# GpSimd multiplies the fourth corner by its weight in every second tap of a deformable convolution's sampling

## The chip, the cores and the metric

The kernel runs on one core of one Trainium2 chip. The metric is the time of one execution on the device, in microseconds (us). Three executions of the kernel before took 7953.55, 7961.13 and 7967.98 us; their median is 7961.13 us. A further one was recorded by the hardware profiler, and all views of the profile come from it.

## The reference

The program is two layers of a vision model on an input of 2 x 128 x 64 x 64 numbers, all float32: a deformable convolution with four branches, a mixture of experts, a state-space mixer and a second mixture of experts, each with a residual. The change lies in the sampling of the deformable convolution. For each branch (kernel sizes 1, 1, 3 and 7) and each of its taps, every output position reads the normalized image at a position that is not whole, as a weighted sum of four neighbours, and the result goes into a product with the tap's weights:

```python
v00 = gather(y0, x0)
v01 = gather(y0, x0 + 1)
v10 = gather(y0 + 1, x0)
v11 = gather(y0 + 1, x0 + 1)
return v00 * (1 - wy) * (1 - wx) + v01 * (1 - wy) * wx + v10 * wy * (1 - wx) + v11 * wy * wx
...
sampled = bilinear_sample(x, py, px) * mask[:, None]
return jnp.einsum('bckhw,ock->bohw', sampled, reg_w.reshape(O, C, k * k))
```

1 + 1 + 9 + 49 = 60 taps are sampled at 4096 positions of each of the two images. The offsets and masks that fix positions and weights come from convolutions of the same image.

## The kernel before

The image lies in device memory as a table (`self.table`) of 67 x 67 rows; a row holds the 4 x 128 channels of the four neighbours of one position, so one gathered row of 2 KB is all that a position needs of a tap. Positions go in groups of 512 (`NG` = 8 groups for an image), a group in `GT` = 4 tiles of 128 positions, one position to a partition. `run` goes through the groups of image 0 and then through those of image 1, and `sample` goes through the 60 taps of a group. That is 2 x 8 x 60 = 960 taps.

In each tap `sample` does the following, in this order:

- GpSimd issues four indirect DMAs (L711), one for each tile. Each gathers 128 rows by the indices `idx` into a buffer `v` of the pool `l0v`, which has six buffers. So the gathers of tap t+6 reuse the buffer of tap t.
- VectorE multiplies the corners 0 and 1 by their weights (L740, 1024 elements for each partition). Then, for two tiles at a time, it multiplies the corners 2 and 3 into a tile `low` (L745) and adds `low` to the corners 0 and 1 (L746), 512 elements each. `low` lies in PSUM, and the weights have been copied there as `pw` (L723), so each of these operations reads SBUF once and PSUM once.
- TensorE transposes both halves of each tile onto the same place in PSUM (L750, eight instructions), which adds them. ScalarE copies the result to `st` (L759; three buffers).
- The product with the tap's weights (L779, in `product`) is put off by two taps, in a list `self.late`. The weights `regw` come in chunks of five taps by a DMA on SP's queue.
- Other work is mixed in by hand, a step for each tap: `conv.step()` advances the offset convolutions of later groups (L402 on TensorE, small operations on VectorE and copies on ScalarE), and `rest.step()` the normalization of image 1, and later the layers that follow for image 0.

The order of each engine's instructions is the order in which the program issues them; no scheduler changes it. Each engine takes its own in that order, and semaphores hold an instruction until what it needs is done. After the sampling, the mixer and the last experts run without the sampling's code.

L431, L433, L440 and L441 are VectorE operations of the offset convolutions that read SBUF twice. L1426, L1331, L1336, L1346, L1365, L1393 and L989 are GpSimd's tensor operations in the mixer and the experts, after the last gather.

Of the kernel before, what the change touches and what calls it, by code (L numbers as in the profile page):

```python
# [10 lines left out]
F32 = mybir.dt.float32  # L11
I32 = mybir.dt.int32
AF = mybir.ActivationFunctionType
ALU = mybir.AluOpType
# [5 lines left out]
P = 128  # L20
B = 2
C = 128
# [3 lines left out]
GT = 4  # L26
# [7 lines left out]
NTAP = len(TAPS)  # L34
FIRST = [0, 1, 2, 11]
NO = 3 * NTAP
TW = H + 3
E0 = 8
E1 = 64
HID = 512  # L40
DS = 16
# [143 lines left out]
class L0Conv:  # L185
# [416 lines left out]
    def run(self, build, after):  # L602

        env, tc, nc = self.env, self.env.tc, self.env.nc
        pools = lambda ctx: lambda name, bufs, **kw: ctx.enter_context(tc.tile_pool(name=name, bufs=bufs, **kw))
        with ExitStack() as ctx:
            pool = pools(ctx)
            self.rp, self.regw = pool("l0rw", 1), {}
            self.ip = pool("l0i", 2)
            self.vp = pool("l0v", 6)  # L610
            self.stp = pool("l0s", 2)
            self.pending = []
            first = ctx.enter_context(ExitStack())
            self.open_offsets(pools(first))
            for i in range(2):
                nc.vector.memset(self.padc[i], 0.0)
            psum = ctx.enter_context(ExitStack())
            right = lambda name: pools(psum)(name, 1, space=PSUM, side="right")
            self.p_f = deque([right("l0po")])
            cur = self.new_group(self.ip)  # L620
            with (
                tc.tile_pool(name="nrm", bufs=3) as sp,
                tc.tile_pool(name="nrmp", bufs=4, space=PSUM) as pp,
            ):
                xs = []
                for g in range(NG):
                    if g % GT == 0:
                        x = self.vp.tile([P, GT, 4 * C], F32, name="v")
                    xs.append(x[:, g % GT, :])
                    nc.sync.dma_start(out=xs[g], in_=env.d["x"][0, :, g * 512 : (g + 1) * 512])  # L630
                xn = self.vp.tile([P, GT, 4 * C], F32, name="v")
                self.load_weights()
                for _ in self.zero_table(0):
                    pass
                own = lambda g: xn[:, g % GT, :].rearrange("p (j c) -> p j c", c=C)
                norms = [self.norm_group(0, g, sp, pp, "nrm", x, own(g)) for g, x in enumerate(xs)]
                together(norms[:2], 2)

                stage = self.rows(0, 0)
                self.sum_weights()  # L640
                others = Side()
                others.add(mixed(norms[2:], 3))
                for _ in range(24):
                    others.step()
                offsets = self.offset_stream([(0, 0, cur)], stage)
                while others.todo:
                    next(offsets)
                    for _ in range(3):
                        others.step()
                self.load_chunk(0)  # L650
                for _ in self.norm_end(0):
                    pass
                for _ in offsets:
                    pass
            self.p_w = pool("l0pw", 1, space=PSUM)
            self.p_r = pool("l0pr", 1, space=PSUM)
            self.p_t = pool("l0pt", 2, space=PSUM)
            self.p_o = pool("l0py", 2, space=PSUM)
            self.pending = [(n, functools.partial(self.load_chunk, c)) for n, c in ((1, 1), (3, 2))]
            early = psum.enter_context(ExitStack())  # L660
            p_m = pools(early)("l0pm", 1, space=PSUM, side="right")

            def more():

                early.close()
                self.p_f.append(right("l0po2"))
                yield


            conv, rest = Side(), Side()  # L670
            self.late, self.made = deque(), [0, 0]
            rest.add(self.norm(1, p_m, "misc"), more(), build)
            ahead = {}

            def runs():
                for g in range(1, NG):
                    ahead[g] = self.new_group(self.ip)
                    yield 0, g, ahead[g]
                    yield 1, g - 1, None
                yield 1, NG - 1, None  # L680

            conv.add(self.offset_stream(runs()))
            for g in range(NG):
                self.sample(0, g, *cur, conv, rest, 2 if g else 3)
                cur = ahead.get(g + 1)
            conv.drain()
            rest.drain()
            psum.close()
            first.close()
            side = ctx.enter_context(tc.tile_pool(name="l0ps", bufs=2, space=PSUM))  # L690
            rest.add(after(0, side))
            cur = self.load_group(1, 0)
            for g in range(NG):
                nxt = self.load_group(1, g + 1) if g + 1 < NG else None
                self.sample(1, g, *cur, conv, rest, 2)
                cur = nxt
            for f in self.late:
                f()
            for _, f in self.pending:
                f()  # L700
            self.pending = []
            rest.drain()

    def sample(self, b, g, idx, w4, conv, rest, pace):

        env, nc = self.env, self.env.nc
        pw, vs = None, {}

        def gather(v, t, tiles):
            for j in tiles:  # L710
                nc.gpsimd.indirect_dma_start(  # L711
                    out=v[:, j, :],
                    out_offset=None,
                    in_=self.table[b],
                    in_offset=bass.IndirectOffsetOnAxis(ap=idx[:, j, t : t + 1], axis=0),
                )

        for br, (k, _) in enumerate(BRANCH):
            for t in range(FIRST[br], FIRST[br] + k * k):
                tw = t % HT  # L720
                if tw == 0:
                    pw = self.p_w.tile([P, GT, HT, 4], F32, name="pw")
                    nc.vector.tensor_copy(pw, w4[:, :, t : t + HT, :])  # L723

                if b == 0 and g == 0 and t == 0:
                    for i in range(6):
                        vs[i] = self.vp.tile([P, GT, 4 * C], F32, name="v")
                        gather(vs[i], i, range(0, 2))
                if t in vs:
                    v = vs.pop(t)  # L730
                    gather(v, t, range(2, GT))
                else:
                    v = self.vp.tile([P, GT, 4 * C], F32, name="v")
                    gather(v, t, range(GT))
                v4 = v.rearrange("p j (q c) -> p j q c", q=4)


                up = v4[:, :, 0:2, :]
                w = pw[:, :, tw, 0:2].unsqueeze(3).to_broadcast([P, GT, 2, C])
                nc.vector.tensor_tensor(up, up, w, ALU.mult)  # L740
                for j in range(0, GT, 2):
                    two = slice(j, j + 2)
                    low = self.p_r.tile([P, 2, 2, C], F32, name="low")
                    w = pw[:, two, tw, 2:4].unsqueeze(3).to_broadcast([P, 2, 2, C])
                    nc.vector.tensor_tensor(low, v4[:, two, 2:4, :], w, ALU.mult)  # L745
                    nc.vector.tensor_tensor(up[:, two], up[:, two], low, ALU.add)  # L746
# [151 lines left out]
class L0Ffn:  # L898
# [3 lines left out]
    def __init__(self, env, dp, wp, gp):  # L902

        nc, d = env.nc, env.d
        self.env, self.dp, self.gp = env, dp, gp
        self.rw = wp.tile([P, E0], F32, name="rw")
        self.rb = wp.tile([P, E0], F32, name="rb")
        self.ew = wp.tile([P, E0 * C], F32, name="ew")
        self.eb = wp.tile([E0, C], F32, name="eb")
        self.tri = wp.tile([P, E0, E0], F32, name="tri")  # L910
        nc.sync.dma_start(out=self.rw, in_=d["router_w"])
# [5 lines left out]
    def group(self, b, g, x1, x2, sp, pp):  # L917
# [19 lines left out]
        yield  # L937
        pl = bank([P, GT, E0], "pl")
        for j in range(GT):
# [620 lines left out]
class L1Ffn:  # L1560
# [8 lines left out]
    def fetch(self, pool):  # L1569

        c = len(self.w1)
        w1 = pool.tile([P, EC, HID], F32, name="wt")
        src = self.env.d["weight1"][c * EC : (c + 1) * EC, 0:C, :].rearrange("e p h -> p e h")
        self.env.nc.sync.dma_start(out=w1, in_=src)
        self.w1.append(w1)
# [8 lines left out]
    def run(self, x3, out):  # L1584
        tc, nc, d = self.env.tc, self.env.nc, self.env.d
        env = self.env
        with ExitStack() as ctx:
# [5 lines left out]
            for b in range(B):  # L1593
                nc.scalar.dma_start(out=w2b[b * E1 : (b + 1) * E1, :], in_=d["weight2"][:, HID, :])
            pq = ctx.enter_context(tc.tile_pool(name="f1q", bufs=1, space=PSUM))
# [309 lines left out]
```

## Time and profile before

| | us |
|---|---|
| median of three executions | 7961.13 |
| the profiled execution | 7970.23 |
| its span (first to last instruction of the program) | 7968.4 |
| PE busy, whole span | 5681.7 (71%) |
| DVE (VectorE) busy | 5782.8 (73%) |
| ACT (ScalarE) busy | 1988.5 (25%) |
| POOL (GpSimd) busy | 4612.1 (58%) |
| first gather, last gather | 108.1, 5808.9 |

A busy time is the sum over the whole span, and a share is a mean over stages with different limits, so the stage of the change must be read by itself. In the window from 112 to 2889 us (image 0) and from 2889 to 5813 us (image 1) the engines were busy as follows; the last columns are the clock granted to TensorE and the share of time in which the 16 DMA engines were busy.

```profile
112.00:2889.00 2777.00, 2092.08 (x9350) 1409.49 (x9350) 2132.12 (x3481) 452.40 (x835) 1801.67 (x1896) 0.86 0.72 222
2889.00:5813.00 2924.00, 2054.01 (x9699) 1340.37 (x9700) 2109.43 (x3031) 540.76 (x1077) 1845.24 (x1941) 0.84 0.74 230
```

The columns with a count are PE, PEld (TensorE's weight loads), DVE, ACT and POOL. A group's line in the profile reads: line, engine, operation, what it writes and reads, shape, count, then busy time and mean length in ns, then the idle time of the engine before these instructions, and what ended most of it. "issue" there means that no wait is seen in the trace.

### The profile page before, as it was taken

Reading aid. Unit: us, or ns where it says so; the run is one execution under the profiler, and the core shown is the slowest. Engines: PE = TensorE matmul, PEld = TensorE weight load, DVE = VectorE, ACT = ScalarE, POOL = GpSimd, SP = SyncE. Lnnn points to the kernel's source line nnn. Section 1 sums busy time; section 2 is a strip of 40 time slices with the busy share of each in tenths; the row PEclk is TensorE's granted clock in tenths of the full one; section 3 lists DMA queues with packets and bytes.
Section 4 is the critical chain, followed back from the end, with each engine's and each line's share of the span. In section 5 each row is a group of like instructions: output and inputs, shape, how many; then the busy total and the mean of one; then the engine's idle time right before and its main releaser. Section 6 shows DMA issues by size and latency. Waiting matters only on the chain. (4 is left out here: it accounts for less than half of the span.)

```text
span 7968.4 us, 77973 instructions
## 1 busy us (share of the span) xinstructions
PE 5681.7 (71%) x25153; PEld 3608.9 (45%) x25153; DVE 5782.8 (73%) x8700; ACT 1988.5 (25%) x3838; POOL 4612.1 (58%) x4589
## 2 busy tenths in 40 slices
PE   4677777777777767767766878765555678756668
PEld 3455555555555534434444656543333456512124
DVE  5877777777777777678787666676756575789982
ACT  1111111111111113211111222211154255455540
POOL 3666666666666666666666666566643334357640
PEclk8888888888888878878888888887787778877789
DMA  7886767677676777877777877777654334434444
GB/s 221 254 270 210 220 206 220 211 215 219 207 221 205 217 226 256 275 237 248 229 239 211 228 208 219 217 217 229 203 163 146 116 99 134 115 128 147 148 136 148
DMA packets 645247, 1597.35 MB, mean 200 GB/s; under 512 B 168020, under 2 KB 253180, under 8 KB 640876
## 3 DMA queue, kind: packets, MB, share of 16 engines
q0 software_dynamic: 307200, 1006.88, 41.6%
q1 hardware_dynamic: 306156, 537.52, 21.4%
q10 hardware_dynamic: 31488, 47.97, 1.7%
q8 instruction: 205, 3.36, 0.2%
q14 instruction: 198, 1.62, 0.1%
HBM read 1478.65 MB, written 115.83 MB: 200 GB/s over the span
## 5 line engine op out<-in xcount | busy, mean ns | idle before, releaser
L711 POOL DMA_INDIRECT v<-table,idx x3840 | 3650.0, 951 | 2123.6 <-issue 1003.8
L779 PE MATMUL out<-st,regw 128*128 128x512 f32 x3840 | 2142.1, 685 | 131.2 <-issue 79.9
L750 PE MATMUL pst<-ident,v 128*128 128x128 f32 x7680 | 1264.9, 306 | 1072.0 <-issue 662.4
L740 DVE TENSOR_TENSOR v<-v,pw 128x1024 f32<-128x1024 f32 x960 | 1168.3, 1217 | 704.2 <-DMA v<-table,idx 566.9
L750 PEld LDWEIGHTS pst<-ident,v 128*128 128x128 f32 x7680 | 1011.9, 158 | 1455.6 <-issue 985.2
L759 ACT COPY st<-pst 128x512 f32<-128x512 f32 x960 | 557.3, 585 | 4350.9 <-remote 2356.1
L746 DVE TENSOR_TENSOR v<-v,low 128x512 f32<-128x512 f32 x1920 | 1318.1, 687 | 68.0 <-remote 1.5
L745 DVE TENSOR_TENSOR low<-v,pw 128x512 f32<-128x512 f32 x1920 | 1328.7, 692 | 33.4
L1426 POOL TENSOR_TENSOR db<-du,bcb 128x512 f32<-128x512 f32 x512 | 657.3, 1289 | 835.4 <-DVE da L1477 683.7
L779 PEld LDWEIGHTS out<-st,regw 128*128 128x128 f32 x3840 | 771.5, 223 | 747.7 <-issue 684.4
L1449 PE MATMUL py<-sc,ident 128*128 128x512 f32 x1024 | 660.6, 751 | 233.0 <-DVE sc L1487 233.0
L1477 DVE TENSOR_TENSOR_SCAN da<-da,state,db 128x512 f32<-128x512 f32 x512 | 657.0, 1283 | 177.9 <-ACT da L1433 134.4
L1449 PEld LDWEIGHTS py<-sc,ident 128*128 128x128 f32 x1024 | 200.2, 229 | 529.3 <-DVE sc L1487 436.2
L402 PEld LDWEIGHTS po<-wa,win 128*128 128x128 f32 x2112 | 330.2, 202 | 141.8 <-issue 141.2
L1152 PEld LDWEIGHTS ps<-ipw,hs 128*120 128x120 f32 x2816 | 343.3, 199 | 109.1 <-issue 75.4
L1487 DVE TENSOR_TENSOR sc<-da,bcb 128x512 f32<-128x512 f32 x512 | 354.2, 692 | 44.8 <-DVE da L1477 1.8
L402 PE MATMUL po<-wa,win 128*128 128x147 f32 x2112 | 358.3, 299 | 35.2 <-issue 34.2
L1152 PE MATMUL ps<-ipw,hs 128*120 128x64 f32 x2816 | 340.8, 281 | 45.3 <-issue 30.8
L1433 ACT ACTIVATE da<-delta,w_A_log 128x512 f32<-128x512 f32 x512 | 354.0, 692 | 18.8 <-DVE delta L1389 2.8
L1160 PEld LDWEIGHTS ps<-tm,X 120*88 120x88 f32 x2048 | 188.7, 170 | 83.7 <-ACT Y L1114 53.3
L1160 PE MATMUL ps<-tm,X 120*88 120x48 f32 x2048 | 195.6, 267 | 41.9 <-ACT Y L1114 37.9
L855 PE MATMUL pfo<-yc,fw 128*128 128x256 f32 x512 | 146.9, 423 | 80.4 <-ACT yc L857 67.3
(296 smaller groups left out, 4695.2 us busy)
## 6 DMA issues: line engine op xcount, KB each, us to landing
bcb<-bc SPq DMA_DIRECT2D x256, 512.0 KB
regw<-in_regw SPq DMA_DIRECT2D x192, 640.0 KB
v<-table,idx POOLq DMA_INDIRECT x3840
yd<-ys ACTq DMA_DIRECT2D x128, 256.0 KB
yc<-yd SPq DMA_DIRECT2D x32, 1024.0 KB
gb<-gd SPq DMA_DIRECT2D x16, 2048.0 KB
wt<-in_weight SPq DMA_DIRECT2D x32, 1024.0 KB
tm<-pos SPq DMA_DIRECT2D x16, 1440.0 KB
```

Of the source, the lines that this page charges most:

```text
L402: m()
L711: nc.gpsimd.indirect_dma_start(out=v[:, j, :], out_offset=None, in_=self.table[b], in_offset=bass.IndirectOffsetOnAxis(ap=idx[:, j, t : t ...
L740: nc.vector.tensor_tensor(up, up, w, ALU.mult)
L745: nc.vector.tensor_tensor(low, v4[:, two, 2:4, :], w, ALU.mult)
L746: nc.vector.tensor_tensor(up[:, two], up[:, two], low, ALU.add)
L750: nc.tensor.matmul(pt[:, j, :], v4[:, j, q, :], env.ident, is_transpose=True, start=j == 0 and q == 0, stop=j == GT - 1 and q == 1,)
L759: nc.scalar.copy(st, pt.rearrange("p j t -> p (j t)"))
L779: nc.tensor.matmul(self.out[half], self.regw[t // CH][:, t % CH, half * P : (half + 1) * P], st, start=first, stop=last,)
L1152: nc.tensor.matmul(ps[:, k, :], patch, own, start=True, stop=True)
L1426: nc.gpsimd.tensor_tensor(dbs[u], pieces[k]["du"][:, half, :], bcb[u // 2][:, 0, :], ALU.mult)
L1449: nc.tensor.matmul(py[k, half], by, what, start=first, stop=last)
L1477: nc.vector.tensor_tensor_scan(s, s, dbs.pop(u), state[:, half, n : n + 1], ALU.mult, ALU.add)
```

## The change

In every second tap of a group (the odd ones; `EVERY` = 2) the fourth corner is multiplied by its weight on GpSimd, in place, with the weight read from `w4` in SBUF. VectorE then does four operations in these taps: the corners 0 and 1 as before, the corner 2 of all four tiles into `low`, its addition to corner 0, and the addition of corner 3 to corner 1, which reads SBUF twice. In the other taps VectorE's five operations stay as they are.

For this the gathers are issued one tap ahead. The gathers of tap t+1 come before GpSimd's product of tap t; `self.held` keeps the buffer until its tap comes, and the last tap of a group issues the gathers of the next group's first one, where its indices exist already (`after`).

```diff
+EVERY = 2
...
-            self.pending = []
+            self.pending, self.held = [], deque()
...
-                self.sample(0, g, *cur, conv, rest, 2 if g else 3)
+                self.sample(0, g, *cur, conv, rest, 2 if g else 3, lambda: ahead.get(g + 1))
...
-                self.sample(1, g, *cur, conv, rest, 2)
+                self.sample(1, g, *cur, conv, rest, 2, lambda: nxt)
...
+        def fetch(idx, t):
+            if t in vs:
+                v = vs.pop(t)
+                self.gather(b, v, idx, t, range(2, GT))
+            else:
+                v = new()
+                self.gather(b, v, idx, t, range(GT))
+            return v
...
+        if not self.held:
+            self.held.append(fetch(idx, 0))
...
-                if t in vs:
-                    v = vs.pop(t)
-                    gather(v, t, range(2, GT))
-                else:
-                    v = self.vp.tile([P, GT, 4 * C], F32, name="v")
-                    gather(v, t, range(GT))
+                if t + 1 < NTAP:
+                    self.held.append(fetch(idx, t + 1))
+                elif after():
+                    self.held.append(fetch(after()[0], 0))
+                v = self.held.popleft()
                 v4 = v.rearrange("p j (q c) -> p j q c", q=4)
+                side = t % EVERY == EVERY - 1
+                if side:
+                    w = w4[:, :, t, 3:4].to_broadcast([P, GT, C])
+                    nc.gpsimd.tensor_tensor(v4[:, :, 3, :], v4[:, :, 3, :], w, ALU.mult)
                 up = v4[:, :, 0:2, :]
                 w = pw[:, :, tw, 0:2].unsqueeze(3).to_broadcast([P, GT, 2, C])
                 nc.vector.tensor_tensor(up, up, w, ALU.mult)
-                for j in range(0, GT, 2):
+                if side:
+                    low = self.p_r.tile([P, GT, C], F32, name="low")
+                    w = pw[:, :, tw, 2].unsqueeze(2).to_broadcast([P, GT, C])
+                    nc.vector.tensor_tensor(low, v4[:, :, 2, :], w, ALU.mult)
+                    nc.vector.tensor_tensor(v4[:, :, 0, :], v4[:, :, 0, :], low, ALU.add)
+                    nc.vector.tensor_tensor(v4[:, :, 1, :], v4[:, :, 1, :], v4[:, :, 3, :], ALU.add)
+                for j in range(0, 0 if side else GT, 2):
                     two = slice(j, j + 2)
                     low = self.p_r.tile([P, 2, 2, C], F32, name="low")
                     w = pw[:, two, tw, 2:4].unsqueeze(3).to_broadcast([P, 2, 2, C])
```

More of the change, by code (lines that the diff above doesn't have):

```diff
@@ L702, in run, with gather, sample @@
             rest.drain()
-    def sample(self, b, g, idx, w4, conv, rest, pace):
+    def gather(self, b, v, idx, t, tiles):
+        for j in tiles:
+            self.env.nc.gpsimd.indirect_dma_start(
+                out=v[:, j, :],
+                out_offset=None,
+                in_=self.table[b],
+                in_offset=bass.IndirectOffsetOnAxis(ap=idx[:, j, t : t + 1], axis=0),
+            )
+    def sample(self, b, g, idx, w4, conv, rest, pace, after):
         env, nc = self.env, self.env.nc
         pw, vs = None, {}
[L709 to L716, printed above, removed]
+        new = lambda: self.vp.tile([P, GT, 4 * C], F32, name="v")
+        def fetch(idx, t):
[6 more added lines that the diff above has]
+            return v
+        if b == 0 and g == 0:
+            for i in range(6):
+                vs[i] = new()
+                self.gather(b, vs[i], idx, i, range(0, 2))
+        if not self.held:
+            self.held.append(fetch(idx, 0))
         for br, (k, _) in enumerate(BRANCH):
@@ L723, in sample @@
                     nc.vector.tensor_copy(pw, w4[:, :, t : t + HT, :])
[L725 to L728, printed above, removed]
-                if t in vs:
-                    v = vs.pop(t)
-                    gather(v, t, range(2, GT))
-                else:
-                    v = self.vp.tile([P, GT, 4 * C], F32, name="v")
-                    gather(v, t, range(GT))
+                if t + 1 < NTAP:
[3 more added lines that the diff above has]
+                v = self.held.popleft()
                 v4 = v.rearrange("p j (q c) -> p j q c", q=4)
+                side = t % EVERY == EVERY - 1
+                if side:
+                    w = w4[:, :, t, 3:4].to_broadcast([P, GT, C])
+                    nc.gpsimd.tensor_tensor(v4[:, :, 3, :], v4[:, :, 3, :], w, ALU.mult)
                 up = v4[:, :, 0:2, :]
```

## The prediction

> **What bounds the kernel now.** I first read the page's groups, to see which engines share the sampling (line numbers are those of the kernel before).
>
> ```profile
> L711 POOL DMA_INDIRECT v<-table,idx x3840 | 3650.0, 951 | 2123.6 <-issue 1003.8
> ...
> L740 DVE TENSOR_TENSOR v<-v,pw 128x1024 f32<-128x1024 f32 x960 | 1168.3, 1217 | 704.2 <-DMA v<-table,idx 566.9
> ...
> L746 DVE TENSOR_TENSOR v<-v,low 128x512 f32<-128x512 f32 x1920 | 1318.1, 687 | 68.0 <-remote 1.5
> L745 DVE TENSOR_TENSOR low<-v,pw 128x512 f32<-128x512 f32 x1920 | 1328.7, 692 | 33.4
> L1426 POOL TENSOR_TENSOR db<-du,bcb 128x512 f32<-128x512 f32 x512 | 657.3, 1289 | 835.4 <-DVE da L1477 683.7
> ```
>
> There are 960 taps, with four gathers each (L711) and 1217 + 2 x 692 + 2 x 687 = 3975 ns of VectorE. The first gather starts at 108 us and the last ScalarE copy of a transposed tap (L759) at 5820 us, so a tap takes some 5.9 us and no engine is full. What the GpSimd gaps are tells the rest: the groups of POOL in the window 112 to 5813 us, then the waits by engine, then the timeline.
>
> ```profile
> L711 POOL DMA_INDIRECT v<-table,idx x3837 | 3646.9, 950 | 2051.2 <-issue 1003.2 <-remote 512.8 <-PE pst L750 286.8
> ```
> ```profile
> ACT st L759 <- remote: 2356.1, 311, 17.8
> ...
> POOL v L711 <- remote: 512.8, 191, 4.8
> POOL v L711 <- PE pst L750: 286.8, 132, 9.6
> DVE v L740 <- DMA v<-table,idx: 566.9, 253, 12.4
> ```
> ```profile
> 2009.31 0.14 PEld L750 LDWEIGHTS pst<-ident,v 128*128 128x128 f32 x1 [1.27 <-issue]
> 2009.59 0.95 POOL L711 DMA_INDIRECT v<-table,idx  x1 [0.30 <-issue]
> ...
> 2010.74 0.14 PEld L750 LDWEIGHTS pst<-ident,v 128*128 128x128 f32 x1 [1.29 <-issue]
> ...
> 2012.17 0.18 PEld L750 LDWEIGHTS pst<-ident,v 128*128 128x128 f32 x1 [1.29 <-issue]
> ...
> 2013.05 0.58 ACT L759 COPY st<-pst 128x512 f32<-128x512 f32 x1 [11.17 <-remote]
> ...
> 2013.23 0.95 POOL L711 DMA_INDIRECT v<-table,idx  x1 [2.70 <-remote]
> ```
>
> A gather is 0.95 us and the next follows 0.30 us later: 1.25 us, 5.0 us a tap. In the window 3836 such gaps of 0.305 us are 1170 us; the rest of the idle 2051.2 us, 881 us, is waiting, most of it put down to "remote", which is a releaser that the trace can't name. The timeline shows what it is: TensorE's transposes come one at a time, 1.4 us apart with no wait named, and the moment ScalarE can copy their result (2013.05), GpSimd's next gather starts (2013.23). The gather of tap t+6 needs the buffer of tap t, which is free when TensorE has transposed it. Counting the 960 L740, L759 and L711 in order, GpSimd waits over 0.3 us in 400 taps, nearly always until within 0.6 us of that copy, and the copy starts 17 us (median) after VectorE is done with its tap. So TensorE's slow stretches set the pace and GpSimd waits 0.92 us a tap. VectorE is mostly early, except for the 253 taps (26%) in which it waits for a gather.
>
> **The change part by part.** The build's instruction lists show the same order on PE, ACT and SP, so only VectorE and GpSimd are costed.
>
> *VectorE.* In each of 480 odd taps five operations become four: the 1217 ns one stays, then 692 (`low`, corner 2), 687 (its addition) and the addition of the fourth corner, from SBUF twice. Its nearest rows are L431 (490 elements, 662 ns) and L433 (476, 649 ns): 0.69 us for 512. That is 3.28 instead of 3.98 us: 0.69 x 480 = 331 us off VectorE. It counts only where VectorE comes last. TensorE's lateness hides most of it; the same count has the next tap already done by VectorE before TensorE delivers the last one in 83% of the taps.
>
> *GpSimd, the product.* 128x512 from two SBUF inputs has many rows: L1426, L1331, L1346, L1365 and L1393 have medians of 1.26 to 1.27 us. The broadcast weight changes little: L989 reads a broadcast too, 2048 elements in 4.50 us, 2.2 ns each against 2.5. I take 1.267 us: 608 us. No tensor operation stands beside a gather in this trace, so the gaps are bounded: products follow each other with none, gathers with 0.30 us. One gap more per product is 0 to 144 us; half, 72 us.
>
> *GpSimd, the gathers.* The new VectorE addition reads SBUF twice. The old ones read PSUM for one input, and gathers beside L745 and L746 take 0.946 us in the mean. Beside two SBUF inputs the timeline has this:
>
> ```profile
> 1086.48 0.66 DVE L431 TENSOR_TENSOR xd<-stage 128x490 f32<-128x490 f32 x1
> 1086.62 1.34 POOL L711 DMA_INDIRECT v<-table,idx  x1 [0.30 <-issue]
> ```
>
> That gather is 0.39 us longer; over all L431, L433, L440 and L441 the mean is 0.15 to 0.21 us per gather met. I take 0.20 us per addition, since an addition that waited for the product starts just as the next gather does: 96 us, bounds 0 and 0.39 x 480 = 187 us.
>
> The Trainium skill ("SBUF — State Buffer", "Who interferes with whom") says that a VectorE instruction with two SBUF inputs contends with a GpSimd one that reads SBUF, and that the later one blocks wholly until the first is done. The row agrees in kind and is smaller; by a full block of 0.69 us the 96 would be 331 us, and POOL's sum 1011 us. The skill also speaks against the change itself ("GPSIMD Engine Reference", "Engine selection"): elementwise work belongs on VectorE, GpSimd being some 2x slower for two inputs. Here 1.267 over 0.69 us is 1.8; at 2x the product would cost 1.38 us, 54 us more in all.
>
> *The moved gathers.* Gathers are issued one tap ahead, so that tap t's product stands behind the four gathers of t+1. No DMA is added. Behind a product on GpSimd's queue stand all gathers from t+2 on; it waits for four landings of tap t, 2.5 us (median) after their issue against 5.0 us of gathers in between, so mostly for nothing. In return a gather that waits for a buffer now also holds the product, and VectorE's last addition behind it.
>
> *The sum.* GpSimd gets 608 + 72 + 96 = 776 us (bounds 608 and 939), 0.81 us a tap, and has 881 us of waiting to put it in. By groups of 60 taps the waiting is 0.71 to 0.84 us a tap from tap 180 to 600 and 0.88 to 1.25 elsewhere; the 105 us left over stay waiting, because there TensorE sets the pace: no gain. The cover is thus nearly used up. It does not fit everywhere: waits come at every third tap or so, products at every second, and where a gather is already what VectorE waits for (26%) the added 1.62 us are late next: 480 x 0.26 x 1.62 = 202 us, less what VectorE saves there, 480 x 0.26 x 0.69 = 86. Of the 116 us left I take half, as TensorE's backlog swallows some: +58 us (between 0 and 116).
>
> The profiled execution, 7970.2 us (a span of 7968.4 and 1.8 around it), becomes 8028; the runs shown have a median of 7961.1, 9.1 lower, so 8019, said as **8020 us**.
>
> **The rivals.**
>
> *Faster.* The waits swallow the product wholly and VectorE's saving shows. For it: 608 us at the lower bound are well under 881. The saving counts where TensorE is not behind, 17% of 960 taps, 163, at 0.69 / 2 us: 56 us, 7905 us. Against it: in most of the stage the waits are no larger than what is added, at the value I take.
>
> *No change.* Both sides cancel: 7961 us. For it: the sum above is zero before the last step.
>
> *Much slower: GpSimd becomes the bound.* In the tap loop it decides from 881 / 480 = 1.84 us per product, all told. The upper bound 939 us is past it, and L1336, the same operation, takes up to 1.75 us in a part of its 32 instances: 0.48 x 480 = 230 us more. 1169 - 881 = +288 us, 8249 us. For it: nothing in this trace shows gathers and products alternating. Against it: the medians at 1.27 us are narrow.
>
> That the change does not do what it says can be left out: the built program holds 480 products on GpSimd, each behind the next tap's gathers.
>
> **How the numbers follow.** The forecast, slower by a little, gets 0.50; much slower 0.14; faster 0.22; no change 0.14. A difference under 0.2% (16 us) can't be told from none in this kernel. So slower 0.64, same 0.14, faster 0.22. The range goes from the faster rival's 7905 to 8165, which holds the forecast with its 0 to 116 us and the nearer part of the much slower case; the likeliest case alone spans 7980 to 8080.
>
> **What would show it.** Right: GpSimd's waits for buffers shrink from 881 to under 200 us, a product of about 1.27 us (x480), gathers with a mean of some 0.97 us, VectorE some 330 us less busy but waiting longer, for gathers and for the product before its last addition. Wrong: waits of several hundred us left on GpSimd with a shorter stage (TensorE's slow stretches got shorter), products well over 1.5 us, or gaps of more than 0.6 us around them.

## The result and the profile after

The changed kernel took 7968.0 us (median of 20 runs, 7942.0 to 7996.6). The kernel before took 7946.9 us beside it on the same chip (20 runs, 7932.2 to 7969.0). The ratio is 1.0025, with a 95% interval of 1.0015 to 1.0036: slower by a quarter of a per cent, 21 us. The profiled spans are 7976.5 us after and 7968.4 us before; these two executions took 10 us more than the median of their kernel and 23 us more, so the two profiles don't show where the 21 us lie.

Line numbers of the changed kernel differ: its gathers are L707, the GpSimd product L750, the corner 0 and 1 product L753, the fourth-corner addition L759, the transposes L769. The kernel before keeps its own (L711, L740, L750) in all its runs. These are groups from the page of the changed kernel:

```profile
L707 POOL DMA_INDIRECT v<-table,idx x3840 | 3808.2, 992 | 1338.1 <-issue 965.2
...
L753 DVE TENSOR_TENSOR v<-v,pw 128x1024 f32<-128x1024 f32 x960 | 1169.3, 1218 | 1058.9 <-DMA v<-table,idx 885.4
...
L750 POOL TENSOR_TENSOR v<-v,w 128x512 f32<-128x512 f32 x480 | 510.3, 1063 | 118.1 <-DMA v<-table,idx 93.5
L759 DVE TENSOR_TENSOR v<-v 128x512 f32<-128x512 f32 x480 | 338.4, 705 | 174.7 <-issue 92.5
```

A product takes 1.063 us, and a gather's mean length rose from 0.951 to 0.992 us. VectorE is busy 5484.1 us in place of 5782.8, and its idle time ahead of the first product of a tap (L753) rose from 704.2 to 1058.9 us, 885.4 of it put down to gathers: what VectorE saved, it now waits. The groups of POOL in the window 112 to 5815 us, which holds the sampling, and then the waits there (engine, what waits, for what: sum, count, longest in us):

```profile
L707 POOL DMA_INDIRECT v<-table,idx x3837 | 3805.2, 992 | 1266.4 <-issue 964.6 <-DMA v<-table,idx 82.3 <-remote 77.5
L750 POOL TENSOR_TENSOR v<-v,w 128x512 f32<-128x512 f32 x480 | 510.3, 1063 | 118.1 <-DMA v<-table,idx 93.5 <-issue 12.9 <-DVE v L765 3.3
```
```profile
DVE v L753 <- DMA v<-table,idx: 885.4, 463, 13.5
...
DVE v L759 <- POOL v L750: 81.8, 78, 3.3
POOL v L707 <- remote: 77.5, 79, 2.8
POOL v L707 <- PE pst L769: 74.7, 57, 5.0
```

GpSimd's new work is 510.3 us of products and 3805.2 - 3646.9 = 158.3 us of longer gathers, 668.6 us. Its idle time in the sampling fell from 2051.2 us to 1266.4 + 118.1 = 1384.5 us, by 666.7 us. The one paid for the other: the waits "remote" and "PE" before a gather were 512.8 and 286.8 us and are 77.5 and 74.7. Where a product meets what stands around it, the timeline shows (start, length, engine, line; in brackets the idle time before):

```profile
2005.60 0.95 POOL L707 DMA_INDIRECT v<-table,idx  x1 [0.31 <-DVE v L758]
...
2006.57 1.06 POOL L750 TENSOR_TENSOR v<-v,w 128x512 f32<-128x512 f32 x1
...
2007.66 0.69 DVE L759 TENSOR_TENSOR v<-v 128x512 f32<-128x512 f32 x1 [2.09 <-POOL v L750]
...
2007.79 1.43 POOL L707 DMA_INDIRECT v<-table,idx  x1 [0.16 <-remote]
```

The product starts 0.02 us after the gather before it, and the next gather follows it after 0.16 us instead of 0.30; these are also the medians over all 480 products. VectorE's last addition waits for the product and starts 0.13 us before that gather, which takes 1.43 us in place of 0.95.

### The profile page after: what moved, and what is told of

Read it like the earlier page. It is cut to its first block, busy times and chain, and to the rows that moved or that the text cites. A ratio compares the mean times of both kernels' runs of the same rounds, so it can differ in the third digit from the quotient of the medians.

```text
span 7976.5 us, 78453 instructions
## 1 busy us (share of the span) xinstructions
PE 5821.2 (73%) x25153; PEld 3638.3 (46%) x25153; DVE 5484.1 (69%) x8220; ACT 1999.1 (25%) x3838; POOL 5281.5 (66%) x5069
## 5 line engine op out<-in xcount | busy, mean ns | idle before, releaser
L707 POOL DMA_INDIRECT v<-table,idx x3840 | 3808.2, 992 | 1338.1 <-issue 965.2
L798 PE MATMUL out<-st,regw 128*128 128x512 f32 x3840 | 2181.1, 694 | 114.5 <-issue 70.9
L769 PE MATMUL pst<-ident,v 128*128 128x128 f32 x7680 | 1302.4, 307 | 978.7 <-issue 706.3
L753 DVE TENSOR_TENSOR v<-v,pw 128x1024 f32<-128x1024 f32 x960 | 1169.3, 1218 | 1058.9 <-DMA v<-table,idx 885.4
L769 PEld LDWEIGHTS pst<-ident,v 128*128 128x128 f32 x7680 | 1007.8, 158 | 1417.5 <-issue 1063.2
L765 DVE TENSOR_TENSOR v<-v,low 128x512 f32<-128x512 f32 x960 | 659.1, 687 | 32.7
L764 DVE TENSOR_TENSOR low<-v,pw 128x512 f32<-128x512 f32 x960 | 664.2, 692 | 16.7
L750 POOL TENSOR_TENSOR v<-v,w 128x512 f32<-128x512 f32 x480 | 510.3, 1063 | 118.1 <-DMA v<-table,idx 93.5
L759 DVE TENSOR_TENSOR v<-v 128x512 f32<-128x512 f32 x480 | 338.4, 705 | 174.7 <-issue 92.5
L758 DVE TENSOR_TENSOR v<-v,low 128x512 f32<-128x512 f32 x480 | 329.7, 687 | 16.3
```

The lines of the kernel that those rows point to most:

```text
L707: self.env.nc.gpsimd.indirect_dma_start(out=v[:, j, :], out_offset=None, in_=self.table[b], in_offset=bass.IndirectOffsetOnAxis(ap=idx[:, ...
L769: nc.tensor.matmul(pt[:, j, :], v4[:, j, q, :], env.ident, is_transpose=True, start=j == 0 and q == 0, stop=j == GT - 1 and q == 1,)
L798: nc.tensor.matmul(self.out[half], self.regw[t // CH][:, t % CH, half * P : (half + 1) * P], st, start=first, stop=last,)
```

## The experiments

Two theories were open. One: GpSimd's added work is the cost, and its waiting for a late TensorE is what hides it. The other: the change acts through something else, the moved gathers, VectorE's new wait or the contention at SBUF.

### Both kernels again, and two parts of the change

The kernel before and the changed kernel, unaltered:

> The kernel before, once more, for a second profile of it and for the spread of the comparison. Both theories: a ratio of 1.000 within 0.0015, and a sampling stage (first VectorE multiplication of corners 0 and 1 to the last copy of a transposed tap) of about 5690 us as in the first profile.

> The changed kernel, once more, for a second profile. Both theories: a ratio of 1.0025 within 0.002. In its first profile the sampling stage was 5 us shorter than before and the part behind it 13 us longer; if the 21 us between the medians lie in the sampling, this profile has a stage longer than 5690 us.

The changed kernel without the GpSimd product; the fourth corner is added unweighted, so this weight is left out:

```diff
                 if side:
-                    w = w4[:, :, t, 3:4].to_broadcast([P, GT, C])
-                    nc.gpsimd.tensor_tensor(v4[:, :, 3, :], v4[:, :, 3, :], w, ALU.mult)
+                    pass
```

> The changed kernel without GpSimd's product: corner 3 of the odd taps stays without its weight; VectorE's four operations, with the addition that reads SBUF twice, stay. Theory A (TensorE and its buffers set the pace of the taps, GpSimd's added work lies in its waits for buffers, and VectorE's saving is worth next to nothing): within 20 us of the kernel before, and so of the changed one; GpSimd waits about 720 us for buffers (881 less the slower gathers). Theory B (the forecast: gathers made late by the product cost time in the 26% of taps where VectorE waits for them, and VectorE's saving counts there): faster than before by 80 us or more (480 x 0.26 x 0.69 = 86).

VectorE's work as before, gathers moved as in the change, and in odd taps a GpSimd product of the same size that waits for no gather and for which nobody waits. It multiplies a tile of zeros and writes bf16 into a tile of its own (only these lines are shown):

```diff
+                if side:
+                    w = w4[:, :, t, 3:4].to_broadcast([P, GT, C])
+                    spare = self.spare.tile([P, GT, C], mybir.dt.bfloat16, name="spare")
+                    nc.gpsimd.tensor_tensor(spare, self.env.zero.rearrange("p (j c) -> p j c", c=C), w, ALU.mult)
```

> GpSimd's product alone, as added work: in the odd taps it multiplies a constant tile by the same broadcast weights into a spare tile that nobody reads, at the place of the product, and it waits for no gather. VectorE does all five operations as in the kernel before. Theory A: the 450 us or so of added GpSimd work vanish in the waits for buffers: within 25 us of the kernel before, GpSimd left with some 400 us of waits. Theory B: the added work passes on to VectorE in 26% of 480 taps, about 0.95 us each, with no saving against it: 60 to 120 us slower.

The expectations were written from the first profile, and this chip gave something else: the kernel before took 7210.2 us here (23 runs, 7195 to 7231), 737 us less than in the first comparison, from the same program.

| | median, us | ratio to the kernel before [95%] |
|---|---|---|
| before_again | 7217.9 | 1.0009 [0.9997, 1.0022] |
| after_again | 7857.2 | 1.0902 [1.0883, 1.0920] |
| no_product | 7202.7 | 0.9984 [0.9973, 0.9995] |
| product_aside | 7593.9 | 1.0533 [1.0513, 1.0554] |

So here the same change costs 9%. What differs is seen in GpSimd's gathers of before_again in its sampling (112 to 5060 us), then in after_again's GpSimd groups (112 to 5692 us):

```profile
L711 POOL DMA_INDIRECT v<-table,idx x3838 | 3644.1, 949 | 1295.6 <-issue 922.0 <-DMA v<-table,idx 136.8 <-PE pst L750 100.8
```
```profile
L707 POOL DMA_INDIRECT v<-table,idx x3839 | 3838.9, 1000 | 1108.5 <-issue 901.4 <-DMA v<-table,idx 151.0 <-DVE v L753 9.1
L750 POOL TENSOR_TENSOR v<-v,w 128x512 f32<-128x512 f32 x480 | 509.2, 1061 | 121.9 <-DMA v<-table,idx 109.6 <-DVE v L765 3.0 <-DVE stats L785 1.3
```

The gathers of the kernel before are as long as in the first profile (949 against 950 ns), but the idle time is 1295.6 instead of 2051.2 us, 755.6 less, and no "remote" is left among the waits named first. GpSimd gathers nearly without a pause: in image 0, 60 taps take 302 us, near the 5.0 us a tap of four gathers, where they took 350 us. With little to hide in, 509.2 + 194.8 = 704.0 us more work took only 65.2 us off the idle time (1108.5 + 121.9 = 1230.4 left); some 62 us of that are the shorter hand-overs, 480 x (0.305 - 0.02 - 0.16). The span grew by 7841.4 - 7216.7 = 624.7 us.

Where the 755.6 us went, TensorE's groups from 400 to 2400 us show, first of the first profile, then of before_again:

```profile
L779 PE MATMUL out<-st,regw 128*128 128x512 f32 x1368 | 779.6, 695 | 63.0 <-issue 45.9 <-ACT ys L793 16.3
L750 PE MATMUL pst<-ident,v 128*128 128x128 f32 x2736 | 448.3, 298 | 327.2 <-issue 288.1 <-DMA v<-table,idx 26.0 <-ACT st L759 5.7
L402 PE MATMUL po<-wa,win 128*128 128x147 f32 x1498 | 256.3, 300 | 26.3 <-issue 25.4 <-DVE v L746 0.7
```
```profile
L779 PE MATMUL out<-st,regw 128*128 128x512 f32 x1604 | 824.6, 640 | 42.6 <-ACT ys L793 37.5 <-DMA regw<-in_regw 5.1
L750 PE MATMUL pst<-ident,v 128*128 128x128 f32 x3212 | 501.4, 288 | 308.2 <-DVE v L746 150.8 <-issue 148.8 <-ACT ys L793 5.2
L402 PE MATMUL po<-wa,win 128*128 128x147 f32 x1772 | 282.9, 291 | 0.0
```

In the first profile TensorE paused for 288.1 us ahead of transposes with no wait named, for 1368 half products; here 148.8 us for 1604, and it waits for VectorE instead. The convolution's matmuls (L402) paused 26.3 us there and not at all here. The granted clock in these 2000 us was 0.86 and 0.94. A tap has four half products, so the 2000 us hold 342 taps there and 401 here. TensorE is busy for 1529.97 and 1648.99 us of them, which makes 4.47 us of work and 1.37 us of pause a tap there, and 4.11 and 0.88 us here.

no_product keeps VectorE's saving and the moved gathers, and gains 0.16%, some 11 us: that is all that VectorE's saving is worth here, net of what its addition does to the gathers (below). product_aside keeps the product and the moved gathers: 7606.3 - 7216.7 = 389.6 us of span for 480 products, 0.81 us each, though nobody waits for them. These are its GpSimd groups (112 to 5432 us):

```profile
L709 POOL DMA_INDIRECT v<-table,idx x3838 | 3670.4, 956 | 1128.9 <-issue 919.8 <-DMA v<-table,idx 95.4 <-DVE low L767 39.2
L753 POOL TENSOR_TENSOR spare<-zero,w 128x512 bf16<-128x512 f32 x480 | 509.0, 1060 | 8.2
```

So most of the cost is GpSimd's time, not VectorE's wait. Neither run gives the whole 624.7 us. Besides VectorE's saving, what the change has beyond product_aside is that the gathers get longer by a further 3838.9 - 3670.4 = 168.5 us, and that the product waits 109.6 us for its own gathers to land, where the spare one sits idle for 8.2 us in all.

In all these runs TensorE isn't late as it was in the first comparison, so for that one the cause is read from its two profiles and from the loaded runs at the end.

### How many products, and the addition's part

Three runs change the number of products, and one takes away the addition that reads SBUF twice. The product in every tap and in every fourth:

```diff
-EVERY = 2
+EVERY = 1
```

> The GpSimd product, the third-corner product and the fourth-corner addition in every tap instead of every second one: 960 products. Theory (GpSimd's work is the cost, TensorE's lateness is the cover): if the kernel before takes about 7210 us on this chip, where the gathers run back to back and 445 products cost 1.43 us each, 960 of them cost about 1370 us: 8580 us, ratio 1.19 (1.17 to 1.20). If the kernel before takes about 7950 us, 960 products take 960 x 0.94 = 902 us and the gathers 1.0 us x a few hundred more, against 881 us of waiting that can be filled: 8100 to 8350 us, ratio 1.02 to 1.05. Rival (the cost is one of moving the gathers one tap ahead and of the order on the engine, not of the products): the ratio stays where it is with 480 products, 1.09 or 1.0025.

```diff
-EVERY = 2
+EVERY = 4
```

> The product in every fourth tap: 240 products. Theory: with the kernel before at about 7210 us, half of the loss of every second tap: 240 x 1.43 = 343 us less what the wait for data can hide, ratio 1.04 to 1.05. With the kernel before at about 7950 us, all of it hidden and 165 us taken off VectorE: ratio 0.997 to 1.002. Rival (order, not products): ratio 1.09 or 1.0025 as with 480 products.

A second product in the same taps:

```diff
                     nc.gpsimd.tensor_tensor(v4[:, :, 3, :], v4[:, :, 3, :], w, ALU.mult)
+                    nc.gpsimd.tensor_tensor(v4[:, :, 3, :], v4[:, :, 3, :], w, ALU.mult)
```

> The changed kernel with the fourth corner multiplied by its weight twice, so that the output holds its square: 960 products in 480 taps, VectorE's work unchanged. Theory: the second product stands back to back with the first and costs its own 1.06 us and no second hand-over: with the kernel before at about 7210 us, 480 x 1.08 = 518 us more than the changed kernel, 8375 us, ratio 1.16. With the kernel before at about 7950 us, 609 + 518 = 1127 us against 881 us of waiting: 246 us too many, ratio 1.03 to 1.045. Rival (VectorE's added wait for the product sets the pace): 480 times the part of 1.08 us by which VectorE is late, on either chip, ratio over the changed kernel's by less than 0.02.

The fourth-corner addition done by TensorE in place of VectorE:

```diff
-                    nc.vector.tensor_tensor(v4[:, :, 1, :], v4[:, :, 1, :], v4[:, :, 3, :], ALU.add)
...
-                    for q in range(2):
+                    qs = (0, 1, 3) if side else (0, 1)
+                    for q in qs:
```

> The changed kernel without the fourth-corner addition on VectorE: TensorE adds it in a third transpose into the same PSUM tile, 4 more transposes in each odd tap. Theory 1 (GpSimd's own product is the cost): with the kernel before at about 7210 us the loss stays near that of a product beside no other change, 1.0 us x 480 = 480 us: 7690 us, ratio 1.06 to 1.075. Theory 2 (the addition that reads SBUF twice costs as much as the product through slower gathers): the gathers' mean falls from 1.00 to 0.95 us, 190 us in all, and the ratio to 1.055 or below. With the kernel before at about 7950 us, 1920 more transposes on an engine that is late: 1.01 to 1.05.

These four ran on another chip, where the kernel before took 7214.5 us. The spans are set beside those of before_again and after_again, which ran on the first of these chips.

| | products | median, us | ratio [95%] | span above before_again, per product |
|---|---|---|---|---|
| every4 | 240 | 7476.6 | 1.0372 [1.0353, 1.0390] | 255.0 / 240 = 1.06 us |
| after_again | 480 | 7857.2 | 1.0902 [1.0883, 1.0920] | 624.7 / 480 = 1.30 us |
| every1 | 960 | 8483.3 | 1.1760 [1.1743, 1.1777] | 1280.1 / 960 = 1.33 us |
| product_twice | 960 in 480 taps | 8380.4 | 1.1607 [1.1584, 1.1630] | 540.5 / 480 = 1.13 us above after_again |
| three_transposes | 480 | 7682.2 | 1.0643 [1.0625, 1.0661] | 464.5 / 480 = 0.97 us |

The loss grows with the number of products, so it isn't one of the moved gathers or of the order, which would have kept the ratio at 1.09. every1 came out below the 8580 us expected: 1.43 us had been put in for each product, and after_again shows 1.37 us in image 0 and 1.30 us over both. The second product of product_twice costs its own length and next to nothing else; if VectorE's wait set the pace, the ratio would have stayed within 0.02 of the changed kernel's, and it's 0.07 above. In product_twice's GpSimd groups (112 to 6215 us) it stands as L751:

```profile
L707 POOL DMA_INDIRECT v<-table,idx x3838 | 3839.6, 1000 | 1107.3 <-issue 830.2 <-DMA v<-table,idx 153.6 <-DVE v L754 19.5
L750 POOL TENSOR_TENSOR v<-v,w 128x512 f32<-128x512 f32 x480 | 507.9, 1058 | 103.6 <-DMA v<-table,idx 94.8 <-DMA regw<-in_regw 1.2
L751 POOL TENSOR_TENSOR v<-v,w 128x512 f32<-128x512 f32 x480 | 504.4, 1051 | 37.6
```

What the addition does to the gathers, three_transposes (112 to 5519 us) and no_product (112 to 5056 us) tell:

```profile
L707 POOL DMA_INDIRECT v<-table,idx x3836 | 3675.1, 958 | 1111.7 <-issue 849.2 <-DMA v<-table,idx 132.3 <-POOL v L750 60.8
```
```profile
L707 POOL DMA_INDIRECT v<-table,idx x3838 | 3703.4, 965 | 1233.7 <-issue 930.1 <-DMA v<-table,idx 142.9 <-DVE v L752 47.3
```

Without the addition the gathers are 3838.9 - 3675.1 = 163.8 us shorter, 0.34 us for each of 480, nearly all of the 175 us by which three_transposes is below after_again. Both theories of that run were partly right: the product is the larger cost, but the addition's hold on the gathers is a quarter of the loss (163.8 of 624.7 us). With the addition but no product, the gathers are only 3703.4 - 3644.1 = 59.3 us longer, 0.12 us for each.

Which of the two starts first decides. From the traces, each gather that overlaps a fourth-corner addition, counted by which began earlier:

| | addition first: gathers, mean us | gather first: gathers, mean us |
|---|---|---|
| after (first comparison) | 346, 1.348 | 135, 0.966 |
| after_again | 421, 1.390 | 85, 0.978 |
| no_product | 224, 1.190 | 345, 0.946 |

A gather that begins beside a running addition is held up: in after_again its median is 1.43 us, with 0.57 us of the addition left. A gather that is already running is hardly lengthened, and the addition beside it isn't either (a median of 0.685 us). An addition that waited for the product starts when GpSimd's next gather is about to start, so it comes first more often, 421 times instead of 224.

### A TensorE that is late on purpose

If a late TensorE is the cover, making it late on a chip where it isn't must make the change cheap again. Both kernels got more transposes of a tile of zeros into each tap's PSUM tile, which leaves the sum as it is:

```diff
-                            stop=j == GT - 1 and q == 1,
+                            stop=False,
...
+                for i in range(18):
+                    nc.tensor.matmul(
+                        pt[:, i % GT, :], env.zero[:, 0:P], env.ident, is_transpose=True, start=False, stop=i == 17
+                    )
```

> The kernel before with 12 more transposes of a tile of zeros into each tap's PSUM tile; the sum is unchanged, TensorE has more to do. In the runs where the kernel before took 7210 us, 8 transposes stand in 0.87 us, so 12 add 1.31 us to the 3.85 us that a tap's TensorE work takes back to back: 5.16 us, beside the 5.0 us of four gathers. Theory (GpSimd's work is the cost, a late TensorE the cover): 7210 to 7500 us, ratio 1.00 to 1.04.

> The changed kernel with the same 12 transposes. TensorE's 5.16 us a tap are still less than the 5.72 us that gathers and products took: theory: 7850 to 8000 us, so that the change still costs 5 to 9 per cent of load12_before. Rival (the change costs the same whatever TensorE does): 9 per cent of load12_before.

> The kernel before with 18 more transposes of zeros a tap: 3.85 + 1.95 = 5.8 us of TensorE a tap, the pace that the kernel before had in its first profile (5.82 us). Theory: TensorE sets the pace, 960 x 0.8 = 770 us more than 7210: 7980 us, ratio 1.10 (1.07 to 1.14), and GpSimd waits some 800 us for buffers that TensorE has not read.

> The changed kernel with the same 18 transposes. Theory (a late TensorE hides GpSimd's product): its 5.72 us a tap fit under TensorE's 5.8 us: within 2 per cent of load18_before, on the same chip on which the change costs 9 per cent without the load. Rival (the change costs the same whatever TensorE does, and the small loss of the first comparison has another cause, such as a slower GpSimd): 7 to 9 per cent above load18_before.

The same with 20, on a further chip:

> The kernel before with 20 transposes of zeros a tap. TensorE was busy 99 per cent of the sampling with 18 (7827 us); 2 more of 0.108 us in 960 taps are 207 us: 8035 us, ratio 1.114 where the kernel before takes 7212 us. If the kernel before takes about 7950 us on this chip, 7950 plus what part of 20 x 0.108 us a tap does not fit into TensorE's unexplained pauses: 8100 to 9500 us.

> The changed kernel with the same 20 transposes. Theory (the loss is what of GpSimd's added 656 us does not fit into its waiting): with 18, its idle time fell by 540 us and 116 us were left over; 20 make some 200 us more room, so all of it fits: load20_before's time within 0.5 per cent. Rival (a part of the loss does not depend on TensorE, because VectorE or TensorE waits for the product): 1.6 per cent above load20_before, as with 18.

The kernel before took 7212.0 and 7221.0 us on these two chips: four chips agree within 0.2%.

| added transposes a tap | before, us | after, us | after / before |
|---|---|---|---|
| 0 | 7210.2 | 7857.2 | 1.0902 [1.0883, 1.0920] |
| 12 | 7409.7 | 7873.9 | 1.063 |
| 18 | 7826.6 | 7950.7 | 1.016 |
| 20 | 7989.7 | 8097.7 | 1.014 |

The last column is the ratio of the two medians where no interval stands; by the outer ends of the two intervals it lies between 1.058 and 1.066, 1.012 and 1.021, and 1.008 and 1.016. load18_before was expected at 7980 us. Its sampling took 5534 / 960 = 5.76 us a tap, near the 5.8 us expected; the 7980 us came from setting this against 5.0 us a tap, where before_again took 4928 / 960 = 5.13. The loss shrinks from 647 to 108 us as TensorE falls behind. In load18_before's sampling (112 to 5665 us) GpSimd now waits for TensorE, and in load18_after's (112 to 5776 us) it has the product there:

```profile
L711 POOL DMA_INDIRECT v<-table,idx x3838 | 3639.7, 948 | 1905.0 <-issue 897.2 <-PE pst L750 736.1 <-DVE v L746 80.8
```
```profile
L707 POOL DMA_INDIRECT v<-table,idx x3838 | 3786.5, 987 | 1255.1 <-issue 873.0 <-PE pst L769 163.7 <-DMA v<-table,idx 137.3
L750 POOL TENSOR_TENSOR v<-v,w 128x512 f32<-128x512 f32 x480 | 508.6, 1060 | 110.0 <-DMA v<-table,idx 99.2 <-DVE v L753 1.5 <-DVE low L764 1.2
```

736.1 us of waiting for TensorE became 163.7. The added work is 508.6 + 146.8 = 655.4 us, the idle time fell by 1905.0 - 1365.1 = 539.9 us, and the difference, 115.5 us, is near the 95.7 us by which the span grew.

That 20 would leave nothing was wrong: 1.4% stayed, by medians. A waiting time summed over the stage doesn't predict that, for with 20 there is more of it than with 18. The loss follows the pace group by group more closely. From the traces, the time from the first L753 (L740) of a group of 60 taps to that of the next (for the last group, to the last copy of a transposed tap), in us; the first column is the mean of image 0's eight groups, the others are those of image 1:

| | image 0 | 9 | 10 | 11 | 12 | 13 | 14 | 15 | 16 | all 16 |
|---|---|---|---|---|---|---|---|---|---|---|
| before (first profile) | 350 | 352 | 369 | 351 | 352 | 375 | 372 | 379 | 340 | 5690 |
| after (first comparison) | 348 | 351 | 376 | 358 | 347 | 387 | 375 | 362 | 342 | 5685 |
| before_again | 302 | 303 | 314 | 329 | 317 | 322 | 321 | 314 | 297 | 4928 |
| after_again | 343 | 345 | 355 | 348 | 349 | 370 | 359 | 350 | 339 | 5560 |
| load20_before | 353 | 347 | 343 | 355 | 327 | 431 | 410 | 353 | 315 | 5707 |
| load20_after | 356 | 344 | 367 | 351 | 346 | 415 | 413 | 368 | 343 | 5799 |

after_again is nearly the pace that GpSimd needs for itself. load20_before is slower than that in image 0 and by far in groups 13 and 14, and faster in groups 10, 12 and 16: there the change loses 24, 19 and 28 us, and the room in groups 13 and 14 can't be used for them. (Group 15 loses 15 us that this doesn't explain.) Taking the slower of load20_before and after_again in each group gives 5768 us against 5799 measured. With 18 transposes it gives 5661 against 5645, with 12 it gives 5570 against 5591, and for the first comparison 5692 against 5685. There the kernel before was already slower than GpSimd's need in nearly every group of both images, so almost nothing was lost.

As a forecast of the loss in the sampling this rule is coarser: 61 us against 92 measured with 20 transposes, 127 against 111 with 18, 455 against 475 with 12, 2 against -5 in the first comparison. It was also found after these runs, not before them. The rival of load20_after, that a part of the loss doesn't depend on TensorE, expected 1.6% and isn't excluded by these loaded runs: image 0 loses 3 us a group with 20 although load20_before is 10 us slower there than after_again. But a fixed part of 1.4% would show in the first comparison too, where the whole loss is 0.25%.

## Why the prediction was right or wrong

- **What bounds the kernel**: that TensorE's slow stretches set the pace, with GpSimd waiting and VectorE early, held for the first comparison. The added transposes show that such a late TensorE makes the change cheap. But the slow stretches weren't a property of the program: on four chips later the kernel before took 726 to 737 us less, and there "GpSimd becomes the bound", the rival at 0.14, was the case from the first product on, not from 1.84 us each.
- **VectorE, 331 us**: right in size. The fourth-corner addition took 0.705 us for 0.69, VectorE was busy 298.7 us less in all, and the saving was hidden as said. On the first of the later chips no_product shows 0.16% where GpSimd has no product.
- **The product, 1.267 us**: too dear. It took 1.063 us, 510 instead of 608 us in all. The rows from the mixer have two whole inputs; the broadcast weight, which was put down as changing little, is the nearest difference, though no run here separates it. L989, the row taken for it, repeats 512 numbers for each expert, while this weight stands for 128 numbers in a row. Two other differences can be left out: product_aside, with another output and no gather behind its input, took 1.060 us, and the 26 L1426 with no VectorE instruction beside them still have a median of 1.264 us. The Trainium skill ("GPSIMD Engine Reference", "Engine selection") has GpSimd about 2x slower for two inputs; here 1.063 us over VectorE's 0.705 us is 1.5.
- **The gaps, 72 us**: none were added. "issue" time on GpSimd went from 1003.2 us to 964.6 + 12.9, 25.7 less; each product put gaps of 0.02 and 0.16 us (medians) in place of one of 0.305.
- **Slower gathers, 96 us**: too low, 158 us, within its bounds of 0 and 187. The reason given, that an addition which waited for the product starts as the next gather does, is what no_product and three_transposes show (0.12 and 0.34 us per addition) and the counts by which one starts first. The page "SBUF — State Buffer" ("Who interferes with whom") calls the shared port pair an exclusive lock. The timeline comes near that: 0.56 us of the addition were left when the gather started, and the gather took 0.48 us longer. It doesn't hold the other way round here, for the additions that started during a gather took 0.685 us in the median.
- **The sum, 776 us**: 510 + 158 - 26 = 642 us. The product was 98 us too dear and the gaps another 98, and that the gathers were 62 us too low, which hid a part of this, is luck. The comparison with 881 us of waiting held, and the remainder was larger than the 105 us given.
- **The step that failed** is the last one, "Of the 116 us left I take half": +58 us where the medians differ by 21 us and the sampling of both images together changed by -5 us in the profiled runs. It charged 1.62 us in each tap in which VectorE waits for a gather, halved for TensorE's backlog, which was far too little. VectorE did wait more for gathers, 885.4 instead of 566.9 us, but the backlog took up nearly all of it. The part behind the sampling took 2148 and 2161 us in these two profiles, and 2140 to 2175 us over all sixteen with no order to it, so the profiles can't tell where the 21 us lie. That the sign was as forecast is therefore no proof of this term. By groups, GpSimd's need with the prediction's own 0.81 us a tap is 60 x (5.0 + 0.81) = 349 us against 340 to 379 us that the groups took anyway. Only groups 1, 4 and 16 (346, 348 and 340 us) are below it, by 13 us together: that comparison would have come near what was measured, and it's the one that the later runs come nearest to.

What stays open is why TensorE paused in the first comparison. The program and its 77,973 instructions are the same, the gathers are as long, and the trace names no wait. The granted clock is lower, 0.86 against 0.94, but the half products are only 695 / 640 = 1.09 times as long; TensorE's work grew by 0.36 us a tap and its pauses by 0.49. The pauses don't come from the lower clock either: of the pauses of over 0.6 us before a weight load with no wait named, 929 of 1111 us in the sampling began while the full clock was granted. Slower loading of instructions isn't seen: the 205 instruction packets of queue q8 took 0.965 us in the median, against 0.961 in before_again. Whether it was the chip or something around it, the runs can't tell: on none of the four chips used later did it come back.

## What to carry to other kernels

Work given to an engine that waits is nearly free only as long as what it waits for stays late, and this has to be asked stretch by stretch: the slower of the two paces in each group came nearer here than one sum of waits for the whole stage. Before building on idle time whose cause the trace can't name, find out whether another chip has it; here the same edit cost 0.25% in one comparison and 9% in another. The operation moved to GpSimd cost its length there, 1.06 us, plus what its consumer, now running as GpSimd's next gather started, added to that gather, 0.34 us in the mean.

## What the hardware showed that was not expected

- The same program took 7947 us in the first comparison and 7210, 7215, 7212 and 7221 us on four chips later. In the profiled runs the sampling differs by 5690 - 4928 = 762 us and the whole span by 751.7 us, so all of it lies in the sampling.
- GpSimd's product in fp32, 128x512 with a broadcast weight, took 1.06 us, where 128x512 with two full inputs took 1.27 us in the mixer. Between gathers it needed less handing over than two gathers need between them: 0.02 us before and 0.16 us after it, against 0.305 (medians).
- A gather that started beside a running addition from two SBUF inputs took 1.39 us in the mean in after_again, in place of 0.95; one that was running when the addition started took 0.98 us, and the addition took 0.69 us in the median either way.
